# Raw values of an attention group stored channel by channel instead of block by block

## The chip, the cores and the metric

The kernel runs on one core of a Trainium2 chip. The metric is the device time of one launch in microseconds (us), the median of several runs. Engines are named as in the profile: PE (matmul; its weight loads are PEld), DVE (vector), ACT (scalar), POOL (GpSimd) and SP, which here only issues DMAs.

## What is computed

One transformer layer: cross-attention with simulated integer quantisation, then a feed-forward block. 1600 query rows (16 x 100) of width 512 attend, in 16 heads of 32 channels, to all 5776 context rows (16 x 361). The parts that matter here, cut from the reference:

```python
def _fq_sym(x, axis):
    s = jnp.maximum(jnp.max(jnp.abs(x), axis=axis, keepdims=True) / 127.0, 1e-08)
    q = jnp.clip(jnp.round(x / s), -127.0, 127.0) * s
...
kv = (cond @ Wkv + bkv).reshape(1, -1, 2, H, hd)
k, v = (kv[:, :, 0], kv[:, :, 1])
...
q = _fq_sym(q, axis=-1)
k = _fq_sym(k, axis=-1)
v = _fq_sym(v, axis=2)
attn = jnp.einsum('bhqd,bhkd->bhqk', q, k)
attn = jax.nn.softmax(attn.astype(jnp.float32), axis=-1)
attn = _fq_unsigned(attn, axis=-1)
out = jnp.einsum('bhqk,bhkd->bhqd', attn, v)
```

Keys get one scale per row and head. Values get one scale per channel, taken over all 5776 rows, so no value can be divided before the last row is projected.

## The kernel before

**Groups and blocks.** The 16 heads form four groups of four heads (128 channels). The context is padded to 46 blocks of 126 rows (plus two spare rows, so 128 partitions). For each group and block the kernel projects keys and values: a 128 x 256 result in PSUM, values in the first 128 columns, keys in the rest. Two blocks form a pair and share one PSUM tile `pp`.

**The array `vraw`** holds what comes out, in fp32, per partition (context row in a block) 50 blocks by 128 channels: 46 blocks of raw values, and four more slots, two pairs deep, for the raw keys of a pair. On a partition the 128 channels of a block lie side by side, and a block follows the one before after 512 B. `vraw` is read and written by these lines, once per pair unless said otherwise:

- L292 `pair_keep`, ACT: copies a pair from PSUM, values to their two blocks, keys to two of the spare slots (512 elements a partition).
- L309, L316, L317 `keys_round`, POOL: multiplies the keys in place by the inverse scale, adds the rounding constant in place, subtracts it and writes bf16 codes (256 elements each).
- L323 `values_max`, DVE: the largest magnitude of each channel over a range of blocks. The plan cuts this into pieces of 256 to 768 elements.
- L353 `values_divide`, POOL: multiplies a range of blocks and channels in place by the inverse channel scale; L356 `values_round`, ACT, then writes them as int8.

**Stages.** In a first stage (to 153 us) the queries and the keys and values of group 0 are made. Then runs the attention loop of 200 tiles, 50 for a group; a tile is one head and 128 query rows. In a tile DVE moves the scores out of PSUM in five chunks and takes the row maximum (L1244), POOL turns the maximum into a bias (L1276, L1287, L1288) and unpacks codes (L1201), ACT takes the exponential twice (L1180) and DMAs transpose the codes. The score array is double buffered by tile. The feed-forward stage follows the loop.

**The next group's keys and values are made inside the loop.** The order on every engine is written out by hand: lists per tile ("pe", "dve", "act", "pool", ...), filled by `put`. `plan_pair` spreads pair u of the next group over tiles 2u to 2u + 3 of the current one: eight projection matmuls (L269) over two tiles, the keys' maximum on DVE (L281) and the copy-out on ACT (L292) at the end of the second, the inverse scale (L304) a tile later, `keys_round` at the start of the next. `pp` has one buffer in the loop (four in the first stage), so the first projection of a pair waits for the copy-out of the pair before. On PE the projections stand in one queue with the score matmuls (L1228), which DVE waits for.

`values_max` stands in tiles 31 to 46 of a group, one piece a tile, at the end of DVE's list. The scale is finished in tiles 47 and 48, and `values_divide` with `values_round` stands in tiles 49 to 65, that is, in the first 15 of the next group; group 3, the last, is divided in tiles 49 to 53. The pieces, as (tile, first block, end block, first channel, end channel):

```python
"divide": (
    (49, 0, 23, 0, HD), (49, 23, NB, 0, HD), (50, 0, 4, HD, P), (51, 4, 8, HD, P), (51, 8, 24, HD, 2 * HD),
    (53, 24, 40, HD, 2 * HD), (55, 40, NB, HD, 2 * HD), (57, 8, 16, 2 * HD, P), (59, 16, 24, 2 * HD, P),
    (61, 24, 32, 2 * HD, P), (63, 32, 40, 2 * HD, P), (65, 40, NB, 2 * HD, P),
),
```

## Time and profile before

| | |
|---|---|
| median of 3 runs | 1866.73 us (1858.79 to 1869.18) |
| the profiled execution | 1868.41 us, its span 1866.6 us |
| first stage | 0 to 153.5 us |
| attention loop, 200 tiles | 153.5 to 1597 us |
| lines that touch `vraw`, busy | L292 53.6, L309 59.0, L316 38.2, L317 37.9, L323 46.1, L353 57.8, L356 26.9 us |

In the lines of the profile, `out<-in` names what an instruction writes and reads, then come the shapes (partitions x elements), the number of instructions, their busy time and the mean time of one in ns, the idle time of the engine before them and what ended it. A line of the table by stretch gives the stretch and its length, then the busy time of each engine. A line of the timeline starts with the start and the duration in us.

### The profile page before, as it was taken

To read this page: it belongs to the slowest core of one execution; us is meant where nothing else is said; L and a number is where in the kernel's file an instruction comes from. 1 tells how busy PE (TensorE), PEld (TensorE's weight loads), DVE (VectorE), ACT (ScalarE), POOL (GpSimd) and SP (SyncE) were. 2 spreads that over 40 slices of the span, in tenths; PEclk is the share of its full clock that TensorE was granted. 3 is DMA by queue.
4 is the path that set the end of the run, shared out by engine and by line. 5 is a ranking of instruction groups with operands and counts; after the bars stand their busy time and mean duration, and the time that the engine had idled before them with its cause. 6 is when DMAs were issued, how large, how long until landed. Compare 5 with 4: busy or idle time off the path is not lost. (4 is left out here: it accounts for less than half of the span.)

```text
span 1866.6 us, 43709 instructions
## 1 busy us (share of the span) xinstructions
PE 1632.8 (87%) x16727; PEld 1147.9 (61%) x16727; DVE 1704.4 (91%) x2944; ACT 1490.1 (80%) x1483; POOL 1316.2 (71%) x1846
## 2 busy tenths in 40 slices
PE   5998898888888988888888888888898898889998
PEld 4985566666555666565656665644555555568776
DVE  7788999999999999999999999998999999888775
ACT  3556899988899999888999998888989887744443
POOL 3557898887788888777898887789767756532211
PEclk9998999999999999999999999999999899989999
DMA  4555999999999999999999999989999999821100
GB/s 145 141 146 116 184 198 216 204 215 198 183 185 201 199 213 203 210 208 182 192 204 207 207 212 203 202 147 197 199 211 201 208 220 226 171 77 35 34 21 21
DMA packets 982448, 323.88 MB, mean 174 GB/s; under 512 B 939943, under 2 KB 946267, under 8 KB 982238
## 3 DMA queue, kind: packets, MB, share of 16 engines
q1 hardware_dynamic: 970428, 300.91, 85.9%
q10 hardware_dynamic: 11810, 20.18, 4.1%
q8 instruction: 131, 2.15, 0.5%
q14 instruction: 79, 0.65, 0.1%
HBM read 79.16 MB, written 10.72 MB: 48 GB/s over the span
## 5 line engine op out<-in xcount | busy, mean ns | idle before, releaser
L1244 DVE TENSOR_SCALAR_CACHE_REDUCE score<-sl 128x1536 f32<-128x1536 f32 (+1 forms) x1000 | 1306.8, 1355 | 67.4 <-PE sl L1228 50.9
L1228 PE MATMUL sl<-kT,qT 96*128 96x512 bf16 (+1 forms) x2304 | 633.0, 371 | 128.9 <-DVE score L1244 122.7
L1180 ACT ACTIVATE pairc<-score,nb,qs 128x2772 uint8<-128x2772 f32 x192 | 518.6, 2701 | 103.8 <-POOL nb L1288 88.6
L1180 ACT ACTIVATE codes<-score,nb,qs 128x3024 uint8<-128x3024 f32 x192 | 558.1, 2907 | 11.3 <-DMA rT<-codes 10.9
L1201 POOL CAST rU<-pk 128x2816 f16<-128x2816 uint8 x200 | 506.1, 2530 | 9.2 <-DMA pk<-pairc 8.1
L269 PE MATMUL pp<-wkv,cb 128*128 128x256 f32 x1104 | 343.1, 392 | 33.6 <-ACT vraw L292 33.2
L1228 PEld LDWEIGHTS <-qT 96*128 96x128 bf16 x2304 | 188.6, 97 | 240.7 <-issue 163.1
L269 PEld LDWEIGHTS pp<-wkv,cb 128*128 128x128 f32 x1104 | 202.5, 191 | 117.4 <-ACT vraw L292 41.5
L1101 PEld LDWEIGHTS <-rT 128*128 128x128 f16 x4608 | 189.7, 96 | 82.9 <-issue 14.6
L1101 PE MATMUL oacc<-v,rT 128*128 128x32 f16 x4608 | 203.7, 177 | 5.5 <-DMA v<-row 3.2
L1287 POOL TENSOR_SCALAR m<-mx,m 128x1 f32<-128x1 f32 x200 | 71.9, 360 | 173.0 <-DVE score L1244 101.8
L1101 PE MATMUL oacc<-v,rU 128*128 128x32 f16 x4224 | 178.8, 177 | 0.0
L1101 PEld LDWEIGHTS <-rU 128*128 128x128 f16 x4224 | 145.1, 96 | 53.7 <-issue 10.4
L935 POOL TENSOR_TENSOR rw<-rl,nw_b 128x480 f32<-128x480 f32 (+3 forms) x39 | 49.6, 1271 | 159.4 <-ACT rl L934 80.4
L917 PE MATMUL p<-w13h,hT 128*128 128x480 f32 (+3 forms) x312 | 123.5, 396 | 4.6 <-ACT hT L902 4.0
L917 PE MATMUL p<-w13l,hT 128*128 128x480 f32 (+3 forms) x312 | 121.4, 389 | 3.2 <-POOL w13l L474 2.8
L292 ACT COPY vraw<-pp 128x512 f32<-128x512 f32 x92 | 53.6, 582 | 59.2 <-DVE am L281 52.0
L397 ACT COPY kT<-kt 96x1008 bf16<-96x1008 bf16 (+2 forms) x97 | 90.6, 934 | 7.7 <-PE kt L393 7.6
L1276 POOL TENSOR_SCALAR m<-mx 128x1 f32<-128x1 f32 x200 | 73.6, 368 | 31.8 <-DVE score L1244 31.5
L309 POOL TENSOR_TENSOR vraw<-vraw,rs 128x256 f32<-128x256 f32 x92 | 59.0, 642 | 40.0 <-DVE rs L304 27.9
L1244 DVE DVE_READ_ACCUMULATOR score<-sl 128x1 f32 x1000 | 82.7, 83 | 0.0
L917 PEld LDWEIGHTS p<-w13h,hT 128*128 128x128 f32 (+1 forms) x312 | 59.8, 192 | 16.7 <-ACT hT L902 6.4
(225 smaller groups left out, 2610.8 us busy)
## 6 DMA issues: line engine op xcount, KB each, us to landing
cb<-in SPq DMA_DIRECT2D x135, 256.0 KB
cr<-in SPq DMA_DIRECT2D x46, 256.0 KB
qT<-q_dram SPq DMA_DIRECT2D x45, 100.0 KB
pk<-pairc SPq DMA_TRANSPOSE x200
rT<-codes SPq DMA_TRANSPOSE x200
xn<-in ACTq DMA_DIRECT2D x12, 256.0 KB
x_s<-in ACTq DMA_DIRECT2D x12, 256.0 KB
x_dram<-x_s ACTq DMA_DIRECT2D x12, 256.0 KB
```

The costliest lines, as they stand in the source:

```text
L269: nc.tensor.matmul(pp, cbs[g, t][:, kb, :], wts_g[g][:, kb, :], start=(kb == 0), stop=False)
L292: nc.scalar.copy(vraw.rearrange("p (u t) c -> p u t c", t=2)[:, u : k + 1 : k - u], pp.rearrange("p t (two c) -> p two t c", two=2),)
L309: nc.gpsimd.tensor_tensor(kv, kv, batch.pop(("rs", g, u)).rearrange("p t h -> p (t h)").unsqueeze(2).broadcast_to([P, 2 * G, HD]), ALU.mult,)
L397: nc.scalar.copy(kT[h][:, c0 * KB : (c0 + n) * KB].rearrange("p (b k) -> p b k", k=KB), exp_.pop(("pt", h, c0))[:, :n, 2:])
L917: nc.tensor.matmul(pt[:r, :w], T["h", t][:, kb, :r], last_w[c][p][:, i * 4 + kb, :], start=(kb == 0 and p == 0), stop=(kb == 3 and p == 1),)
L1101: nc.tensor.matmul(oacc[h][:, t, :], turned(n, bl), v16[h][:, bl, :], start=(bl == turns[0]), stop=(bl == turns[-1]),)
L1180: nc.scalar.activation(dst, src, AF.Exp, bias=nb, scale=s1, accum_out=usum[:, i, n % 50 : n % 50 + 1])
L1201: nc.gpsimd.tensor_copy(r.rearrange("p (b two) q -> p b two q", two=2), packed.pop(n).bitcast(U8).rearrange("p b (q two) -> p b two q", tw ...
L1228: nc.tensor.matmul(sl[:, x0:x1], qT[h][:, t * P : (t + 1) * P], kT[h][:, col + x0 : col + x1], start=True, stop=True,)
L1244: nc.vector.tensor_scalar(sc[:, col : col + w], sl[:, :w], 1.0, None, ALU.mult, ALU.max, accum_out=mx[:, c : c + 1])
L1276: nc.gpsimd.tensor_scalar(m1, mx[:, 0:1], mx[:, 1:2], mx[:, 2:3], ALU.max, ALU.max)
L1287: nc.gpsimd.tensor_scalar(m2, mx[:, 3:4], mx[:, 4:5], m1, ALU.max, ALU.max)
```

## The change

`vraw` is allocated as 128 channels by 50 blocks on each partition, and every use sees it through a view with blocks and channels swapped. The 50 blocks of a channel lie side by side (4 B apart) and the next channel follows after 200 B. `keys_round` names blocks and heads as two axes, since they no longer merge into one. All other lines keep their text and go through the view.

```diff
-    vraw = genp.tile([P, NB + 4, P], F32, name="vraw")
+    vraw = genp.tile([P, P, NB + 4], F32, name="vraw").rearrange("p c t -> p t c")
...
     def keys_round(g, u):
         k = NB + (2 * u) % 4
-        kv = vraw[:, k : k + 2, :].rearrange("p t (h d) -> p (t h) d", d=HD)
+        kv = vraw[:, k : k + 2, :].rearrange("p t (h d) -> p t h d", d=HD)
         nc.gpsimd.tensor_tensor(
             kv,
             kv,
-            batch.pop(("rs", g, u)).rearrange("p t h -> p (t h)").unsqueeze(2).broadcast_to([P, 2 * G, HD]),
+            batch.pop(("rs", g, u)).unsqueeze(3).broadcast_to([P, 2, G, HD]),
             ALU.mult,
         )
```

The order in which an instruction walks its elements stays: L292, L309, L316, L317, L353 and L356 run over channels innermost, L323 over blocks innermost.

## The prediction

> **What bounds the kernel now.** I read the page's first part, then the table of busy time by stretch, then the groups of instructions by shape, then the timeline at one pair of blocks.

> ```profile
> span 1866.6 us, 43709 instructions
> PE 1632.8 (87%) x16727; PEld 1147.9 (61%) x16727; DVE 1704.4 (91%) x2944; ACT 1490.1 (80%) x1483; POOL 1316.2 (71%) x1846
> ...
> core 0: us, PE busy (x) PEld busy (x) DVE busy (x) ACT busy (x) POOL busy (x), PEclk, DMA share, GB/s
> ...
> 80.00:100.00 20.00, 20.00 (x147) 18.62 (x146) 17.34 (x38) 12.22 (x23) 11.32 (x18) 1.00 0.61 170
> ...
> 740.70:858.60 117.90, 102.06 (x1206) 70.05 (x1204) 117.03 (x192) 103.38 (x85) 93.32 (x143) 1.00 1.09 203
> 883.10:995.20 112.10, 98.53 (x1166) 68.12 (x1164) 107.57 (x177) 106.92 (x96) 101.28 (x146) 1.00 1.06 196
> ```

> The columns after the length are PE, PEld, DVE, ACT and POOL. The first stage (to 153 us) is PE's: 20.00 of 20.00. In the attention loop DVE sets the pace, but by two regimes. In tiles 31 to 46 of a group (740.70:858.60) DVE is busy 117.03 of 117.90 us and POOL and ACT have room. In tiles 50 to 65 (883.10:995.20), when the finished values are divided and rounded, DVE, ACT and POOL are all above 90%: ACT idles 5.2 us in 112.1, POOL 10.8.

> ```profile
> L292 ACT COPY vraw<-pp 128x512 f32<-128x512 f32 x92 | 53.6, 582 | 59.2 <-DVE am L281 52.0 <-DVE sd L552 2.5 <-PE kt L393 2.3
> L353 POOL TENSOR_TENSOR vraw<-vraw,tops 128x512 f32<-128x512 f32 x19 | 24.3, 1279 | 0.9
> L323 DVE TENSOR_REDUCE tops<-vraw 128x16 f32<-128x480 f32 x24 | 22.6, 942 | 0.0
> L948 DVE TENSOR_REDUCE tiny<-kb 128x1 f32<-128x480 f32 x24 | 15.7, 653 | 0.8
> ```

> L323 and L948 reduce the same 480 fp32 numbers on the same engine; L323 reads them 512 B apart and takes 942 ns, L948 reads them side by side in 653. So this trace prices a far step on DVE.

> ```profile
> 289.40 0.42 DVE L281 TENSOR_REDUCE am<-pp 128x8 f32<-128x256 f32 x1
> 289.88 1.70 DVE L1244 TENSOR_SCALAR_CACHE_REDUCE score<-sl 128x1536 f32<-128x1536 f32 x1
> 289.91 0.59 ACT L292 COPY vraw<-pp 128x512 f32<-128x512 f32 x1 [0.71 <-DVE am L281]
> 290.55 0.70 PE L269 MATMUL pp<-wkv,cb 128*128 128x256 f32 x2 [0.37 <-ACT vraw L292]
> 291.08 0.60 PE L1228 MATMUL sl<-kT,qT 96*128 96x512 bf16 x2
> 291.72 1.22 DVE L1244 TENSOR_SCALAR_CACHE_REDUCE score<-sl 128x1024 f32<-128x1024 f32 x1
> ```

> This is the chain that matters, once per pair of blocks: DVE's maximum L281 lets ACT copy the pair out (L292), the copy frees the one pp buffer, PE's next projection (L269) waits 0.37 us for it, and the score matmuls queued behind it (L1228) reach DVE late. The first chunk ends at 291.58 by its row, the next starts at 291.72: with the accumulator read between them about 0.2 us are lost already. The copy has no slack here.

> **The change, part by part.** The built program keeps every instruction, every engine's order and every wait; nothing is added, removed or moved past a queue, no DMA touches vraw. Only the address steps of seven lines differ: each now steps 200 B from element to element (50 fp32 of a channel), except L323, whose reads become contiguous. So the whole effect is in durations.

> *Values maximum, L323 (DVE, gains).* Per group of the loop, eight of 480 elements go from 942 to L948's 653 ns: 8 x 0.289 = 2.3 us. Two of 512 go from 999 to 686 (L880, 512 contiguous): 0.6. Two of 384 go from 784 to 554 (L948's 620 ns at 448 elements less 64 x 1.03): 0.5. The one of 256 takes 0.37 already and stays. Sum 3.4 us, in tiles 31 to 46, where DVE has no idle: on the path. Three groups: -10.2 us. The first group's reductions fall in the first stage, under PE's 20.00 of 20.00, and count nothing; if PE had room they would bring some 4 us.

> *Copy-out, L292 (ACT).* It now writes 200 B apart; no row shows a strided fp32 write. Lower bound 0: the steps only grow, and a gain from that has no reason. Upper bound from DVE's rows: L323 takes 1518 ns for 768 elements and 999 for 512, 2.03 ns an element, where L948 takes 1.03 (653 at 480, 620 at 448), so a far step costs one more element time. ACT's element time is (977 - 766) ns / 252 = 0.84 ns (L397 at 1008 and 756 elements), so 512 x 0.84 = 0.43 us. I take 0.43, because DVE's strided read is the nearest row. Of 23 pairs in a group, the eight beside L323 (tiles 31 to 46) are covered: there DVE runs 0.95 us more before its next chunk, 0.66 after the change, and 0.43 + 0.2 still fits. The other 15 pay in full: behind the copy wait PE's projection and its score matmuls, and DVE waits for those. 15 x 3 x 0.43 = +19.4 us. Without L323's cover it would be 30.

> *Keys, L309, L316, L317, and division, L353 (POOL).* POOL's slope for a contiguous copy is (400 - 343) / 64 = 0.89 ns (L384 at 256 and 192). Lower bound 0; upper bound a full second pass for each strided read and for each strided write: L309 and L353 double their 2.13 ns an element (L353: 1279 at 512, 1749 at 736), L316 pays 0.46, L317 0.23: 1.24 us a pair. I take one element time per instruction, again by DVE's row: 3 x 0.23 = 0.68 us a pair, and 0.89 ns per divided element.

> *Rounding, L356 (ACT).* It reads 200 B apart: by the same step 0.84 ns an element, 0 as the lower bound.

> These two are hidden where POOL and ACT idle (tiles 16 to 48: POOL idles 24.6 us in 740.70:858.60). In tiles 50 to 65 they are not. The plan divides 4416 of a group's 5888 elements there and finishes eight pairs. ACT: 106.9 + 8 x 0.43 + 4416 x 0.84 ns = 114.0 us. POOL: 101.3 + 8 x 0.68 + 4416 x 0.89 ns = 110.7. The copy's stalls stretch the 112.1 us by 3.4 to 115.5, leaving ACT 1.5 us of idle where it has 5.2 now. ACT waits in turn for POOL's bias and holds DVE's score buffer, so I let it keep its idle: +3.5 us a group, +10.5. Group 3's values are all divided in tiles 149 to 153 (1226.6:1275.9, ACT 45.2 of 49.3 us busy): ACT gets 5888 x 0.84 ns = 4.9 us, of which I count 4. In the first stage ACT (12.2 of 20) and POOL (11.3 of 20) hide their extra 10 and 16 us behind PE: +1.

> Sum: -10.2 + 19.4 + 10.5 + 4 + 1 = +24.7 us. The profiled execution took 1868.4 us (span 1866.6 and 1.8 around it), 1.7 above the median of three: 1866.7 + 24.7 = 1891.4.

> [...] L323's smallest form reads two blocks 512 B apart, 256 elements, and takes only 0.37 us, less than L281's 0.42 for 256 contiguous ones: coming back to a place after two steps cost nothing there. [...]

> **Rivals.**

> *Strides cost ACT and POOL nothing.* For it: the 0.37 us row, and POOL's L309 at 2.4 ns an element, far slower than DVE, may hide an address step. Against: the 942 ns row. Then only L323 changes: -10.2, 1856.5 us. This is the case on the other side.

> *Only POOL pays.* For it: a write may be buffered where a read isn't; then L292 stays 582 and no chain stalls. In tiles 50 to 65 POOL gets 9.3 us against 10.8 of idle, of which 0.48 a tile goes between instructions even in 289.88:296.67, where it is never free (6.31 of 6.79 busy): 3 to 5 us spare, so about +5 a group. -10.2 + 15 + 3 = +8, 1875 us.

> *POOL pays for reads and writes.* 8 x 1.24 + 4416 x 2.13 ns = 19.3 us in tiles 50 to 65; less 3.4 of stretch and 4 spare, POOL becomes the bound by 12 a group in place of ACT's 3.5: +25 on the sum, 1917 us.

> **How the numbers follow.** The forecast has 0.55, its own range 1878 to 1908 (the copy between 0.25 and 0.55 us, the tight stage between 0 and +8 a group). Nothing paid: 0.15. Only POOL: 0.15. POOL twice: 0.15. A range that keeps 8 in 10 reaches down just short of the first rival and up past the last: 1859 to 1922. This kernel's measurement tells about 0.5%, 9.3 us, from no change. The free case sits at -10.2, hardly beyond it: 0.11 faster. Its rest and most of "only POOL" give 0.18 the same. Slower 0.71.

> **What would show it.** L323 at 480 elements near 653 ns; L292 near 1.0 us; L316 and L317 near 0.63, L309 near 0.85, L353 near 1.73 at 512, L356 near 1.04. "PE pp waits for ACT vraw" should grow from 33 to some 60 us, DVE's wait for PE's score tiles from 51 to about 70, and 740.70:858.60's counterpart should shrink by about 3 us. L292 still at 0.58 us sinks the forecast at once; POOL's lines above twice their time point to the last rival.

## The result and the profile after

| | before | after |
|---|---|---|
| median of 4 runs | 1867.88 us (1858.79 to 1869.18) | 1943.20 us (1935.82 to 1948.03) |
| ratio, 95% interval | | 1.0411 [1.0363, 1.0458] |
| span of the profiled execution | 1866.6 us | 1946.2 us |
| mean granted clock | 0.977 | 0.954 |

The change makes the kernel 4% slower. The direction was forecast, but the loss is three times the sum: the span grew by 79.6 us where 24.7 were worked out, and the time lies above the whole range. The first lines of the page, and the view of the cores with span and granted clock:

```profile
span 1946.2 us, 43709 instructions
PE 1668.5 (86%) x16727; PEld 1162.1 (60%) x16727; DVE 1697.0 (87%) x2944; ACT 1551.5 (80%) x1483; POOL 1391.2 (71%) x1846
```

```profile
core 0: 1946.2 us, clock 0.954
```

The same view before:

```profile
core 0: 1866.6 us, clock 0.977
```

The number of instructions is the same to the last one. ACT is busy for 61 us more and POOL for 75; DVE, which set the pace, for 7 us less, and its share fell from 91% to 87%: it waits more. The groups by shape, with the lines the prediction priced:

```profile
L292 ACT COPY vraw<-pp 128x512 f32<-128x512 f32 x92 | 102.7, 1116 | 63.4 <-DVE am L281 54.3 <-DVE sd L552 4.0 <-DMA xn<-in 2.2
L309 POOL TENSOR_TENSOR vraw<-vraw,rs 128x256 f32<-128x256 f32 x92 | 70.7, 768 | 34.1 <-DVE rs L304 24.9 <-ACT sd L548 6.9 <-ACT vraw L292 2.0
L316 POOL TENSOR_SCALAR vraw<-vraw 128x256 f32<-128x256 f32 x92 | 65.4, 711 | 8.4
L317 POOL TENSOR_SCALAR kb<-vraw 128x256 bf16<-128x256 f32 x92 | 61.2, 666 | 7.9
L353 POOL TENSOR_TENSOR vraw<-vraw,tops 128x512 f32<-128x512 f32 x19 | 29.3, 1543 | 0.9
L356 ACT CAST v<-vraw 128x512 int8<-128x512 f32 x19 | 21.6, 1137 | 0.0
L323 DVE TENSOR_REDUCE tops<-vraw 128x16 f32<-128x480 f32 x24 | 14.9, 622 | 0.0
```

Four of these lines before the change:

```profile
L309 POOL TENSOR_TENSOR vraw<-vraw,rs 128x256 f32<-128x256 f32 x92 | 59.0, 642 | 40.0 <-DVE rs L304 27.9 <-ACT sd L548 9.9 <-ACT vraw L292 2.0
L316 POOL TENSOR_SCALAR vraw<-vraw 128x256 f32<-128x256 f32 x92 | 38.2, 415 | 8.4
L317 POOL TENSOR_SCALAR kb<-vraw 128x256 bf16<-128x256 f32 x92 | 37.9, 412 | 7.9
L356 ACT CAST v<-vraw 128x512 int8<-128x512 f32 x19 | 11.7, 617 | 0.0
```

The copy-out went from 582 to 1116 ns, the three keys' steps together from 1.47 to 2.15 us a pair, and the maximum over 480 elements from 942 to 622. The two waits of the forecast (time in total, times, longest):

```profile
DVE score L1244 <- PE sl L1228: 115.9, 149, 4.6
...
PE pp L269 <- ACT vraw L292: 70.0, 66, 3.2
```

The first is DVE's wait for PE's scores, the second PE's wait for the copy-out. They were 50.9 and 33.2 us before. PE's wait came out near the forecast 60; DVE's wait, forecast at 70, grew by 65 us where PE's grew by 37. So DVE lost more than the copy's delay. The table by stretch shows where. The columns are as before; the first two lines answer to 740.70:858.60 and 883.10:995.20 (tiles 31 to 46 and 50 to 65 of the same groups), the last three are one tile each, with the same work in three groups:

```profile
785.20:904.70 119.50, 101.98 (x1206) 69.78 (x1204) 114.48 (x192) 106.31 (x85) 98.61 (x142) 0.99 1.02 192
929.30:1056.90 127.60, 109.05 (x1167) 72.50 (x1165) 107.88 (x177) 115.32 (x96) 108.32 (x146) 0.91 0.95 181
...
320.80:329.90 9.10, 7.73 (x74) 5.09 (x72) 6.68 (x12) 7.69 (x6) 6.57 (x11) 0.81 1.05 223
704.40:711.80 7.40, 6.03 (x73) 4.38 (x71) 6.63 (x12) 7.00 (x5) 6.50 (x11) 1.00 1.14 229
1086.60:1094.00 7.40, 6.04 (x73) 4.38 (x72) 6.63 (x12) 6.99 (x5) 6.51 (x11) 1.00 1.08 227
```

In the tight stage (929.30:1056.90) no engine is full: ACT has 12 us of idle in 127.6, POOL 19, DVE 20. What differs is the granted clock, 0.91 where it was 1.00. And of the three tiles with the same work, the one with the clock at 0.81 takes 9.10 us, the two others 7.40. The timeline at the pair shows both losses. First tile 70, at full clock:

```profile
704.53 1.12 ACT L292 COPY vraw<-pp 128x512 f32<-128x512 f32 x1 [0.31 <-DVE am L281]
705.70 0.70 PE L269 MATMUL pp<-wkv,cb 128*128 128x256 f32 x2 [0.91 <-ACT vraw L292]
706.24 0.60 PE L1228 MATMUL sl<-kT,qT 96*128 96x512 bf16 x2
706.87 1.23 DVE L1244 TENSOR_SCALAR_CACHE_REDUCE score<-sl 128x1024 f32<-128x1024 f32 x1 [0.76 <-PE sl L1228]
```

The copy ends 0.53 us later than before, PE's projection waits 0.91 us instead of 0.37, and DVE's second chunk waits 0.76 us where it lost 0.23 in most such tiles. That is the forecast chain, with the copy's growth passed on in full. Then tile 20, the same four steps:

```profile
320.97 1.12 ACT L292 COPY vraw<-pp 128x512 f32<-128x512 f32 x1 [0.31 <-DVE am L281]
322.14 1.13 PE L269 MATMUL pp<-wkv,cb 128*128 128x256 f32 x2 [0.91 <-ACT vraw L292]
323.07 1.06 PE L1228 MATMUL sl<-kT,qT 96*128 96x512 bf16 x2
324.16 1.23 DVE L1244 TENSOR_SCALAR_CACHE_REDUCE score<-sl 128x1024 f32<-128x1024 f32 x1 [1.60 <-PE sl L1228]
```

The wait is the same 0.91 us, but behind it two projections take 1.13 us instead of 0.70 and two score matmuls 1.06 instead of 0.60: from 322.3 to 325.7 PE runs at half clock. DVE now waits 1.60 us, and again before the third chunk. The half-clock stretches are 3.41 us long or a multiple of it. In tiles 5 to 149 there are 4 of them before (20.5 us in all) and 21 after (102.4 us).

**Where the 79.6 us went.** The PE time lost to the clock is length times (1 - granted clock). Over the span it was 1866.6 x 0.023 = 42.9 us before and 1946.2 x 0.046 = 89.5 after: +46.6. In tile 20 the loss was 9.10 x 0.19 = 1.73 us, and the tile took 1.65 us longer from chunk to chunk than tiles 70 and 120, so I count it one to one. The table counts 0.53 us for each pair whose copy is not covered, and 0.2 us for each of the 18 pairs beside the maxima, which is what their tiles show; the maxima's gain is by L323's rows. The last column is what is left.

| part | change | clock | copy stalls | maxima | left |
|---|---|---|---|---|---|
| first stage | +7.1 | +1.7 | | | +5.4 |
| tiles 0 to 30 | +18.4 | +8.6 | +8.0 | | +1.8 |
| tiles 31 to 48, 81 to 98, 131 to 148 | +7.7 | +8.5 | +6.9 | -11.4 | +3.7 |
| tiles 49 to 66, 99 to 116 | +30.0 | +21.7 | +8.4 | | -0.1 |
| tiles 67 to 80, 117 to 130 | +9.0 | +4.0 | +7.4 | | -2.4 |
| tiles 149 to 158 | +8.5 | +4.2 | | | +4.3 |
| from tile 159 | -1.2 | -2.1 | | | +0.9 |
| sum | +79.5 | +46.6 | +30.7 | -11.4 | +13.6 |

Two causes make most of the loss: the longer copy, 30.7 us where 19.4 were forecast, and a lower clock, which the forecast did not have at all. The sum leaves 13.6 us to neither. This is an accounting; the experiments test it. The clock is the profile's two decimals, so a row is good to some 1 to 2 us (the clock of the last row is the difference to the whole span).

The clock's 46.6 us come from one execution of each kernel. Over all executions on record the loss to the clock is 35 to 54 us for the kernel before (41 executions, median 47) and 79 to 90 for the changed one (4, median 86), so by the medians it grew by 40. Nor does one to one hold everywhere: among the 41 executions the time rises by only 0.4 us for each us lost, among the four of the changed kernel by 1.1. So the clock's share of the 79.6 us is an estimate, some 40 to 47 us if each us counts in full.

### The profile page after: what moved, and what is told of

Read it like the earlier page. It is cut to its first block, busy times and chain, and to the rows that moved or that the text cites. A ratio compares the mean times of both kernels' runs of the same rounds, so it can differ in the third digit from the quotient of the medians.

```text
span 1946.2 us, 43709 instructions
## 1 busy us (share of the span) xinstructions
PE 1668.5 (86%) x16727; PEld 1162.1 (60%) x16727; DVE 1697.0 (87%) x2944; ACT 1551.5 (80%) x1483; POOL 1391.2 (71%) x1846
## 3 DMA queue, kind: packets, MB, share of 16 engines
q8 instruction: 131, 2.15, 0.4%
## 5 line engine op out<-in xcount | busy, mean ns | idle before, releaser
L1244 DVE TENSOR_SCALAR_CACHE_REDUCE score<-sl 128x1536 f32<-128x1536 f32 (+1 forms) x1000 | 1312.0, 1356 | 148.5 <-PE sl L1228 115.9
L1228 PE MATMUL sl<-kT,qT 96*128 96x512 bf16 (+1 forms) x2304 | 651.1, 380 | 121.3 <-DVE score L1244 115.1
L269 PE MATMUL pp<-wkv,cb 128*128 128x256 f32 x1104 | 361.7, 410 | 70.0 <-ACT vraw L292 70.0
L1228 PEld LDWEIGHTS <-qT 96*128 96x128 bf16 x2304 | 187.7, 98 | 236.1 <-issue 162.5
L269 PEld LDWEIGHTS pp<-wkv,cb 128*128 128x128 f32 x1104 | 212.4, 201 | 162.0 <-ACT vraw L292 77.4
L292 ACT COPY vraw<-pp 128x512 f32<-128x512 f32 x92 | 102.7, 1116 | 63.4 <-DVE am L281 54.3
L397 ACT COPY kT<-kt 96x1008 bf16<-96x1008 bf16 (+2 forms) x97 | 90.8, 936 | 7.7 <-PE kt L393 6.9
L309 POOL TENSOR_TENSOR vraw<-vraw,rs 128x256 f32<-128x256 f32 x92 | 70.7, 768 | 34.1 <-DVE rs L304 24.9
L1244 DVE DVE_READ_ACCUMULATOR score<-sl 128x1 f32 x1000 | 83.2, 83 | 0.0
L316 POOL TENSOR_SCALAR vraw<-vraw 128x256 f32<-128x256 f32 x92 | 65.4, 711 | 8.4
```

What stands on the lines that cost most here:

```text
L269: nc.tensor.matmul(pp, cbs[g, t][:, kb, :], wts_g[g][:, kb, :], start=(kb == 0), stop=False)
L292: nc.scalar.copy(vraw.rearrange("p (u t) c -> p u t c", t=2)[:, u : k + 1 : k - u], pp.rearrange("p t (two c) -> p two t c", two=2),)
L309: nc.gpsimd.tensor_tensor(kv, kv, batch.pop(("rs", g, u)).unsqueeze(3).broadcast_to([P, 2, G, HD]), ALU.mult,)
L397: nc.scalar.copy(kT[h][:, c0 * KB : (c0 + n) * KB].rearrange("p (b k) -> p b k", k=KB), exp_.pop(("pt", h, c0))[:, :n, 2:])
L1228: nc.tensor.matmul(sl[:, x0:x1], qT[h][:, t * P : (t + 1) * P], kT[h][:, col + x0 : col + x1], start=True, stop=True,)
L1244: nc.vector.tensor_scalar(sc[:, col : col + w], sl[:, :w], 1.0, None, ALU.mult, ALU.max, accum_out=mx[:, c : c + 1])
```

## The experiments

All times are compared with the kernel before on the same chip (medians 1865.9 to 1869.5 us). "Lost to the clock" is span x (1 - granted clock), in us, as above.

| run | median us | ratio, 95% interval | span | lost to the clock |
|---|---|---|---|---|
| before | 1867.88 | | 1866.6 | 42.9 |
| after | 1943.20 | 1.0411 [1.0363, 1.0458] | 1946.2 | 89.5 |
| e1_fill_wait | 1930.03 | 1.0345 [1.0315, 1.0376] | 1928.5 | 55.9 |
| e2_scores_first | 1900.13 | 1.0170 [1.0139, 1.0200] | 1899.4 | 62.7 |
| e3_old_layout_far_copy | 1905.69 | 1.0217 [1.0184, 1.0250] | 1899.5 | 60.8 |
| e4_before_scores_first | 1860.95 | 0.9972 [0.9951, 0.9993] | 1858.3 | 44.6 |
| e5_old_layout_far_keys | 1899.46 | 1.0168 [1.0151, 1.0185] | 1899.0 | 62.7 |
| e6_old_layout_far_divide | 1930.11 | 1.0342 [1.0313, 1.0371] | 1924.8 | 80.8 |
| e7_new_layout_keys_apart | 1890.93 | 1.0125 [1.0110, 1.0140] | 1888.1 | 58.5 |
| e8_new_layout_copy_by_pairs | 1889.56 | 1.0118 [1.0097, 1.0139] | 1886.3 | 60.4 |
| e9_new_layout_near_walks | 1885.27 | 1.0103 [1.0085, 1.0120] | 1884.2 | 60.3 |
| e10_near_walks_scores_first | 1872.89 | 1.0045 [1.0028, 1.0063] | 1867.2 | 56.0 |
| e11_old_layout_far_round_reads | 1881.20 | 1.0065 [1.0041, 1.0089] | 1880.5 | 47.0 |
| e12_far_copy_fill_wait | 1910.31 | 1.0234 [1.0216, 1.0252] | 1910.6 | 42.0 |

### Does PE's wait bring the clock down?

**e1_fill_wait.** The changed kernel, with six extra score matmuls on PE ahead of the projection that waits for the copy. They go into the second chunk's tile, which the true ones overwrite.

```diff
+                        if c == 0 and n % 2 == 0 and 0 < n < NTI - 50 and t < NT - 1:
...
+                            for i in range(6):
+                                nc.tensor.matmul(
+                                    early_sl[0][:, 0:512],
+                                    qT[h][:, t * P : (t + 1) * P],
+                                    kT[h][:, col : col + 512],
...
```

> The changed kernel with six more score matmuls issued on PE just before the first projection of an even tile (they write the next score chunk's tile and are overwritten), so PE works while it waits for the copy-out. The copy itself and DVE's wait for it stay. Theory of the clock: PE's wait, now about 0.5 us longer per pair, pulls the granted clock to half in some 20 more stretches of the loop, and each costs 1 to 2 us; with the wait filled those stretches fall from about 24 (tiles 5 to 150) to under 10, and the time falls by 25 to 40 us, to 1905-1918. Rival, full engines: the loss is ACT's and POOL's longer work, and the slow stretches only follow from it; then the time stays within 8 us of 1943.

Measured: 1930.0 us, 13 below the changed kernel, between the two theories' numbers. The clock did what the theory says: the prices on ACT and POOL stayed (the copy took 1115 ns), and the loss to the clock fell from 89.5 to 55.9 us; the half-clock stretches in tiles 5 to 149 went from 21 to 5. But the filler has a price of its own. An undisturbed tile with a pair grew from 7.46 to 7.60 us, tile 16 from 8.78 to 9.25, and the span fell by only 17.7 us of the 33.6. So the run shows that PE's idle time in that wait brings the clock down, and not, by its time, what the clock costs.

**e12_far_copy_fill_wait** asks the same on the old layout: e3 (below) plus the filler.

> The old layout with the far copy (1905.7) and the six filling matmuls on PE. The copy's stall of DVE stays, the clock is held. Theory of the clock: the slow stretches of tiles 5 to 150 fall from 12 to under 5 and the time by 8 to 15 us, to 1891-1898. Rival: the stretches are harmless, the time stays within 4 us of 1905.

Measured: 1910.3 us, 4.6 above e3, which is the rival's side. Here too the loss to the clock fell, from 60.8 to 42.0, no more than before the change; the stretches went from 12 to 3. The undisturbed pair grew from 7.39 to 7.60 us, tile 16 from 8.71 to 9.25, and tiles 159 to 199, all in the last group, which holds no filler, took 7.5 us more than in e3, 2.3 of it by the clock and the rest for a reason not found. The filler gave back all it had gained. As a test of the clock's price by total time it failed; tiles with equal work, like 20 and 70 above, are the better measure.

### What does the copy alone cost?

**e3_old_layout_far_copy.** The kernel before, with only the copy's walk changed: heads innermost, so that each element is written 128 B from the one before, and read from PSUM 128 B from the one before.

```diff
-            vraw.rearrange("p (u t) c -> p u t c", t=2)[:, u : k + 1 : k - u],
-            pp.rearrange("p t (two c) -> p two t c", two=2),
+            vraw.rearrange("p (u t) (h d) -> p u t d h", t=2, d=HD)[:, u : k + 1 : k - u],
+            pp.rearrange("p t (two h d) -> p two t d h", two=2, d=HD),
```

> The kernel before, old layout, with one change: the copy-out walks the channels in steps of 128 B (heads innermost), in PSUM and in vraw alike. Keys, maxima, division and rounding are as before. It measures what a slow copy does alone. Both theories: the copy goes from 0.58 to about 1.1 us. Theory of the clock: +24 us of direct stalls (45 pairs by 0.53) and 15 to 30 us of slow clock: 1905-1922. Rival, full engines: without POOL's and the rounding's longer work the tight stage still fits, so +24 at most: 1885-1892.

Measured: 1905.7 us, at the near end of the theory's range; the copy took 1060 ns. An undisturbed pair took 7.39 us with 0.69 of wait before the second chunk (before: 6.93 and 0.23), and the loss to the clock rose by 17.9 us. So a far copy alone costs 39 us, twice what the prediction gave to it, and part of that is the clock.

**e8_new_layout_copy_by_pairs.** The changed kernel, with the copy walking the two blocks innermost: two elements that lie 4 B apart are written in a row, then the next channel.

```diff
-            vraw.rearrange("p (u t) c -> p u t c", t=2)[:, u : k + 1 : k - u],
-            pp.rearrange("p t (two c) -> p two t c", two=2),
+            vraw.rearrange("p (u t) c -> p u c t", t=2)[:, u : k + 1 : k - u],
+            pp.rearrange("p t (two c) -> p two c t", two=2),
```

> The changed kernel with the copy-out walking the two blocks of a pair innermost: two neighbours of 4 B are written before the step of 200 B (PSUM is read in steps of 1 KB in turn). [...] If the reads from PSUM in far steps cost the same, or each write counts by itself, the copy stays at 1.0 to 1.2 us and the time at 1943.

Its copy among the groups by shape, and its timeline at the pair in tile 70:

```profile
L292 ACT COPY vraw<-pp 128x512 f32<-128x512 f32 x92 | 58.5, 636 | 53.8 <-DVE am L281 46.1 <-DVE sd L552 2.8 <-POOL stack L386 2.0
```

```profile
680.14 0.64 ACT L292 COPY vraw<-pp 128x512 f32<-128x512 f32 x1 [0.24 <-DVE am L281]
...
680.84 0.70 PE L269 MATMUL pp<-wkv,cb 128*128 128x256 f32 x2 [0.43 <-ACT vraw L292]
...
682.01 1.23 DVE L1244 TENSOR_SCALAR_CACHE_REDUCE score<-sl 128x1024 f32<-128x1024 f32 x1 [0.28 <-PE sl L1228]
```

The same bytes at the same far places cost 636 instead of 1116 ns once neighbours are written in a row (the reads from PSUM, now in steps of 1 KB, add at most the 54 ns over the 582 of before), and the chain is back at 0.43 and 0.28 us. The time fell to 1889.6, 54 us under the changed kernel. Its span is 59.9 us shorter: 29.1 by the clock, 51 x 0.48 = 24.5 by the uncovered pairs, and the first stage is 5.8 shorter, 1.7 of it by the clock: 57.7 together. Tiles 31 to 48 of the three groups are 3.5, 3.0 and 2.7 us shorter than before the change. That is the gain of the maxima, which the changed kernel gave back to stalls and clock.

**e2_scores_first.** The changed kernel, with the second chunk's score matmuls put ahead of the waiting projection in even tiles, so that DVE no longer waits behind it.

```diff
+EARLY = (("turn", 6), ("unit", "unit", 3), ("unit", 20), ("unit", 7), (10,))
...
-                for what in (WINDOWS if n < NTI - 50 else LAST["windows"])[n % 2][c]:
+                own = (WINDOWS if n < NTI - 50 else LAST["windows"])[n % 2]
+                if 0 < n < NTI - 50 and n % 2 == 0:
+                    own = EARLY
+                for what in own[c]:
```

> The changed kernel, but in even tiles the score matmuls of the second chunk stand on PE ahead of the pair's first projection instead of behind it. This takes the copy-out off DVE's path and keeps PE busy for part of the wait. Theory of the clock: DVE's gap before the second chunk (0.77 us in most even tiles) goes to 0.1 or less and most slow stretches go with it: 1880-1895. Rival, full engines: only the direct stalls go, some 20 us: 1915-1925.

Measured: 1900.1 us, between the two, nearer the theory. DVE's waits before the second chunk of even tiles (2 to 148) fell from 69.5 to 2.5 us in all, and the loss to the clock from 89.5 to 62.7. The copy is as long as in the changed kernel (1115 ns); 43 us of the change's loss went away with the order on PE alone.

**e4_before_scores_first.** The same edit on the kernel before.

> The control of the run with the scores first, on the kernel before: the same reordering on PE, nothing else. Both theories: DVE's gap of 0.23 us in 15 even tiles a group goes, 8 to 12 us less if nothing else is upset: 1855-1862; no change or a small loss if the two projections in a row make the third chunk late.

Measured: 1860.9 us in 10 runs, 0.28% under the kernel before, with an interval that ends below 1. It is the fastest version found and beats both kernels, by little: before the change each pair had only 0.23 us to give.

### What do the keys cost POOL?

**e5_old_layout_far_keys.** The kernel before, with the three keys' steps walking heads innermost, 128 B apart.

```diff
-        kv = vraw[:, k : k + 2, :].rearrange("p t (h d) -> p (t h) d", d=HD)
+        kv = vraw[:, k : k + 2, :].rearrange("p t (h d) -> p t d h", d=HD)
...
-        nc.gpsimd.tensor_scalar(kint[g][:, 2 * u : 2 * u + 2, :], raw, -MAGIC, 1.0, ALU.add, ALU.mult)
+        nc.gpsimd.tensor_scalar(kint[g][:, 2 * u : 2 * u + 2, :].rearrange("p t (h d) -> p t d h", d=HD), raw, -MAGIC, 1.0, ALU.add, ALU.mult)
```

> The kernel before, old layout, with the keys' rounding on POOL (three instructions a pair) walking heads innermost in steps of 128 B; copy, maxima, division and rounding of values as before. Theory A, the copy is most of the loss and POOL's price is hidden where POOL idles: three instructions together 0.5 to 0.9 us longer per pair, time at most 8 us up, 1867-1875. Rival B, POOL in the tight stage is as costly as the copy: 15 to 25 us up, 1882-1892.

Measured: 1899.5 us, +32, above both ranges. The size was missed by the edit itself: the bf16 codes are here written far apart as well, which the change does not do, and that made L317 twice as long as in the changed kernel (666 ns):

```profile
L317 POOL TENSOR_SCALAR kb<-vraw 128x256 bf16<-128x256 f32 x92 | 125.2, 1361 | 7.9
```

The three steps cost 1.38 us more a pair, against 0.68 in the change. So the run shows that POOL's keys are not free and that they too bring the clock down (19.7 us more lost), but not the change's own amount.

**e7_new_layout_keys_apart.** The changed kernel, with the raw keys in an array of their own, contiguous; the copy becomes two instructions.

```diff
+    kraw = genp.tile([P, 4, P], F32, name="kraw")
...
+        nc.scalar.copy(kraw[:, 2 * (u % 2) : 2 * (u % 2) + 2, :], pp[:, :, P:])
+        nc.scalar.copy(vraw[:, 2 * u : 2 * u + 2, :], pp[:, :, 0:P])
```

> The changed kernel with the raw keys in an array of their own, side by side as before; the copy-out is two instructions (keys, then values in far steps). Takes away POOL's price for the keys alone, the copy stays about as long (0.37 contiguous and 0.7 far by half of 1.12 and a fixed part). Theory A: the copy stays the cost, time within 10 us of 1943. Rival B: 15 to 25 us less, 1918-1928.

Measured: 1890.9 us, 52 us under the changed kernel, more than expected. The copy halves take 369 and 617 ns, the pair's wait before the second chunk is 0.52 us instead of 0.76 (51 x 0.24 = 12 us), the first stage is 8.5 us shorter, and the loss to the clock is 31.0 us less. POOL's steps are back at 642, 422 and 411 ns. Taking away the copy's excess (e8) or the keys' price with a little of the copy (e7) each brings over 50 us, though the change costs 75 in all: the two meet in the same loss to the clock, 29.1 and 31.0 of the 46.6 us.

### What do division and rounding cost?

**e6_old_layout_far_divide.** The kernel before, with both walking the blocks innermost.

```diff
-        v = vraw[:, t0:t1, c0:c1]
-        by = fin["rsvb"][:, c0:c1].unsqueeze(1).broadcast_to([P, t1 - t0, c1 - c0])
+        v = vraw[:, t0:t1, c0:c1].rearrange("p t c -> p c t")
+        by = fin["rsvb"][:, c0:c1].unsqueeze(2).broadcast_to([P, c1 - c0, t1 - t0])
...
-        nc.scalar.copy(v8[:, t0:t1, c0:c1], vraw[:, t0:t1, c0:c1])
+        nc.scalar.copy(v8[:, t0:t1, c0:c1].rearrange("p t c -> p c t"), vraw[:, t0:t1, c0:c1].rearrange("p t c -> p c t"))
```

> The kernel before, old layout, with division (POOL) and rounding (ACT) of the values walking blocks innermost in steps of 512 B, 128 B in the int8 output; copy, keys and maxima as before. Theory A: only the tight stages feel it, 3 to 6 us a group and as much in the last division: 12 to 20 us up, 1879-1887. Rival B, the copy's and this cost only hurt together because each alone still fits in ACT's idle time: under 6 us up, 1867-1873.

Measured: 1930.1 us, above both ranges, and no measure of the change, for its rounding also writes its int8 128 B apart:

```profile
L356 ACT CAST v<-vraw 128x512 int8<-128x512 f32 x19 | 48.3, 2541 | 0.0
```

2541 ns, where the changed kernel takes 1137 and the kernel before 617. The division took 1368 ns at 512, near the kernel before (1279).

**e11_old_layout_far_round_reads** mends that: only the rounding's reads are far (16 B steps), its writes contiguous.

```diff
-        nc.scalar.copy(v8[:, t0:t1, c0:c1], vraw[:, t0:t1, c0:c1])
+        nc.scalar.copy(
+            v8[:, t0:t1, c0:c1].rearrange("p t (b a) -> p t b a", b=4),
+            vraw[:, t0:t1, c0:c1].rearrange("p t (a b) -> p t b a", b=4),
+        )
```

> [...] The channels of a group's values come out in another order within each piece, which leaves the output different and the work the same. It asks who owns the 20 us that remain with the near walks. Theory A, the rounding: L356 goes from 0.62 to about 1.1 us for 512 elements, and the time rises by 10 to 18 us, to 1877-1885, all of it in tiles 49 to 66 of a group, 0 to 16 and the last division (149 to 158). Rival B, the rounding hides in ACT's idle time and the rest is POOL's: L356 as long, the time at most 5 us up.

Measured: 1881.2 us, +12, the theory's number. The rounding took 1117 ns at 512, within 2% of the change's. Tiles 49 to 66 and 99 to 116 grew by 3.9 and 3.4 us and tiles 149 to 158 by 5.7: the sizes that the prediction gave to the tight stage and the last division. But 5.1 of the 7.3 us in the tight stages and 2.8 of the 5.7 are clock; over the whole span the loss to the clock rose by 4 us only, because from tile 159 on it is 8.2 us less than in the profile before. So the theory's number was met in part by the clock, which the theory did not have.

### Can the new layout be made to pay?

**e9_new_layout_near_walks.** e8, with the keys' in-place steps by pairs as well, and the division along the blocks of a channel.

```diff
-        kv = vraw[:, k : k + 2, :].rearrange("p t (h d) -> p t h d", d=HD)
+        kv = vraw[:, k : k + 2, :].rearrange("p t (h d) -> p h d t", d=HD)
...
-        nc.gpsimd.tensor_scalar(raw, raw, MAGIC, 1.0, ALU.add, ALU.mult)
+        nc.gpsimd.tensor_scalar(kv, kv, MAGIC, 1.0, ALU.add, ALU.mult)
```

> The changed kernel with three walks turned so that neighbours in memory are touched in a row: the copy-out by pairs (as in the run before, 1889.6), the keys' two in-place steps by pairs, the division along the blocks of a channel. The keys' last step and the rounding keep their far reads. What is left of the change's loss (about 22 us) then tells its owner. Theory A, POOL's price is the rest: copy 0.64, keys' in-place steps back to 0.62 and 0.40, division at 1.28 for 512, time 1865-1875. Rival B, the rounding on ACT is the rest (0.52 us per 512 elements, some 5 us in each tight stage): at most 8 us under 1889.

Measured: 1885.3 us, only 4 under e8, as the rival had it. The division fell to 1077 ns at 512 and L316 to 464, but the multiplication of the keys by pairs got dearer than far apart:

```profile
L309 POOL TENSOR_TENSOR vraw<-vraw,rs 128x256 f32<-128x256 f32 x92 | 97.4, 1059 | 28.6 <-DVE rs L304 23.2 <-ACT sd L548 3.6 <-ACT vraw L292 1.5
...
L353 POOL TENSOR_TENSOR vraw<-vraw,tops 128x512 f32<-128x512 f32 x19 | 20.5, 1077 | 0.9
```

The keys' sum is 2.20 us a pair against 2.15 in the changed kernel, so that part was not improved; the rounding stayed at 1144 ns.

**e10_near_walks_scores_first.** e9 with the order of e2.

> The same with the second chunk's scores ahead of the first projection in even tiles. It is the candidate to beat both kernels: the shorter maxima bring 10 us, the reordering 6, the far reads that are left cost about 10: 1855-1865, against 1861 for the reordering on the old layout.

Measured: 1872.9 us in 9 runs, above the expected numbers. The new layout at its best here is 0.45% slower than the kernel before and 12 us slower than e4.

## Why the prediction was right in direction and wrong in size

**Right: nothing but durations.** The same 43709 instructions run in the same order, and the chain from the maximum over the copy and the projection to DVE's second chunk is the one that was read in the profile before. e8 shows it from the other side: a short copy alone puts it back.

**Right: the prices of DVE and, in sum, of POOL's keys.** L323 at 480 elements took 622 ns (forecast near 653); by the rows of all its sizes a group gains 8 x 0.32 + 2 x 0.34 + 2 x 0.26 = 3.8 us where 3.4 were worked out. The keys cost 2.15 - 1.47 = 0.68 us a pair, as forecast, but that is luck: L309 took less (768 ns, not 850), L316 and L317 more (711 and 666, not 630), and the errors cancel. The division was cheaper, 1543 ns at 512 instead of 1730.

**Mis-sized: the copy.** 1116 ns against "near 1.0 us": a far write costs ACT 0.53 us on 512 elements, where 0.43 was taken as the upper bound from DVE's reads. ACT's far reads cost about the same, 0.52 us: L356 took 1137 ns against 617, for a forecast 1040. What matters to ACT's writes here is shown by e8: with the two neighbours of a pair, 4 B apart, written in a row the copy took 636 ns, with the same two 128 steps apart 1116. The 0.37 us row, a read of DVE that is back after two steps, stays unexplained.

**Mis-counted: the cover.** "The eight beside L323 (tiles 31 to 46) are covered" held for six, those in tiles 32 to 40 and 46, and about 0.2 us of each still came through. In tiles 42 and 44 the pair paid in full, so 17 pairs of a group paid, not 15. The maxima do not stand in every tile from 31 to 46: the plan has 13 pieces there and none in tiles 41 to 43, so nothing covered these two. With 0.53 us each, the term of +19.4 became 51 x 0.53 + 18 x 0.2 = 30.7 us.

**Failed: the sum has no term for the clock.** The step "15 x 3 x 0.43 = +19.4" priced a stall at its own length, and "So the whole effect is in durations" left the clock as it was, without a reason. What the runs showed in its place is that a longer wait of PE also costs granted clock, and that the work behind it then takes longer (at the clock of 0.50 in tile 20 two projections 1.13 us instead of 0.70, two score matmuls 1.06 instead of 0.60): 46.6 us more lost than before in the profiled executions, more than all other terms together. Filling the wait (e1) took 33.6 of it away. The kernel before showed a lowered clock already: 0.977 over its span, 42.9 us lost. The stretches that the prediction shows have a clock of 1.00, the fourth that it used, 1226.60:1275.90, has 0.97, and tiles 0 to 4 would have warned that the clock is not given:

```profile
153.50:197.80 44.30, 33.01 (x184) 19.76 (x185) 35.68 (x60) 30.59 (x32) 29.62 (x53) 0.85 0.66 129
```

The 0.85, behind the five engines, is the clock, in a stretch where PE is busy for 33 of 44 us. The code warned too: it has matmuls that only keep PE busy (`keep_warm`, `keep_busy`). No long pause of PE stands ahead of most drops: the waits of tile 20 are those of tile 70, where PE is idle for 1.37 us of 7.40 in all, at most 0.91 at once, and before 13 of the 21 drops of the changed kernel in tiles 5 to 149, PE was never idle for 1 us at once in the 3.41 us ahead.

**Why tile 20 drops and tile 70 does not.** Their waits are the same; the traces show what differs. Within a trace the half-clock stretches start on one fixed grid of 3.41 us. The table by stretch, along that grid, before and behind the drop in tile 20, then for the same work at tile 70:

```profile
318.85:322.27 3.42, 1.84 (x22) 1.18 (x19) 3.42 (x6) 2.93 (x3) 3.22 (x4) 1.00 1.02 254
322.27:325.68 3.41, 3.41 (x11) 1.76 (x12) 1.52 (x4) 3.31 (x3) 3.03 (x7) 0.50 1.26 231
701.15:704.56 3.41, 2.74 (x41) 1.97 (x40) 3.41 (x8) 3.10 (x5) 3.32 (x3) 1.00 0.91 204
704.56:707.97 3.41, 2.50 (x21) 1.69 (x19) 2.65 (x3) 3.14 (x2) 2.92 (x8) 1.00 1.22 240
```

**The tight stage.** It was forecast to end at 115.5 us with ACT nearly full, +3.5 us a group beside the stalls. It took 127.6, and by the table its whole growth of 30.0 us in two groups is clock (21.7) and copy stalls (8.4). Nothing is left for the load on ACT and POOL (in tiles 0 to 30, which hold group 0's division, at most 1.8). e11, which adds the rounding's load alone, has 3.9 and 3.4 us there, but without the clock only 2.2 of these 7.3 are left. So no run shows the +3.5 us a group as time by itself. Nor are the clock's 21.7 us the copy's alone: the loss to the clock there grew by 3.4 with the far copy alone (e3), still by 8.5 without the copy's excess (e8), and by 18.8 in e6, whose copy is as before. One half-clock stretch of 3.41 us is 1.7 us of this.

**First stage and last division.** The first stage was given +1 and took +7.1. It is PE's only in its middle: PE's projections of the context (L529) wait 9.6 us in all for `cl`, where they waited 4.1, and POOL and DVE, which make it (L520), wait for ACT. With the short copy of e8 the stage grew by 1.3 us, with the keys apart (e7) by nothing, with a far copy alone (e3) by 3.1, with far keys alone (e5), dearer than the change's, by 7.3: ACT's copy and POOL's keys each can lengthen the stage, and the split between them was not measured. The last division was given +4 and grew by 8.5, of which the clock has 4.2; the forecast's part held.

**The rivals.** "Strides cost nothing" and "only POOL pays" fell with the copy's 1116 ns. "POOL pays for reads and writes", 1917 us, came nearest in time but not in cause: the keys cost POOL 0.68 of its 1.24 us a pair and the division 0.52 of its 2.13 ns an element, and POOL idles 19 us in the tight stage. (L309's 642 ns for 256 elements are 2.5 ns an element, not the 2.4 of the first rival.)

**What stays open.** What decides between 52% and 63% of PE's busy time was not found out, and no run shifted the grid or lengthened the wait by steps. Nor is it shown how much of the time lost to the clock is lost to the kernel: filling the wait had a price of its own, and the executions give 0.4 to 1.1 us for each us.

## What to carry to other kernels

When a change lengthens a wait of PE, read the granted clock of each stretch first, and carry a term for it: here 51 pairs with 0.53 us more of stall cost 27 us, and the clock, by the estimate above, another 40 to 47. When a layout is turned, turn the walks with it, so that each instruction touches neighbours in a row; for the copy-out this was two letters of a pattern and worth 54 us. Measure each one, though: POOL's product of two tensors got dearer that way. What a reader gains by a layout (11 us on DVE here) is to be weighed against every writer and reader whose walk stays as it was.

## What was not expected of the hardware

Small types written far apart were dear: int8 at 128 B steps took ACT 2541 ns for 512 elements against 617, of which far reads alone explain 500 (1117 in e11), and bf16 at 64 B steps took POOL 1361 ns for 256 against 412, where far reads alone gave 666. On POOL walking in pairs helped the operation with a constant (L316 711 to 464 ns) and harmed the one with two tensors (L309 768 to 1059; its second operand was walked in another order too), while long runs along a channel made the division faster than in the old layout (1077 ns against 1279). And half clock came with PE's waits below 1 us, after 3.41 us in which PE was still busy for 54% (tile 20).
